# A graph kernel's gather stage: count matrices made four sets ahead instead of two, and gates of groups worked one by one in one PSUM bank

## The chip, the cores and the metric

The kernel runs on one core of a Trainium2 chip. The metric is the device time of the whole program in microseconds, the median of several runs. The kernel before took 1409.13 us (three runs: 1401.07, 1409.13 and 1409.19).

## The reference

The reference takes 6250 nodes of 256 features (`x`) and 100000 edges, sorted by one end (`src`, `dst`). Cut to what matters:

```python
xn = _layernorm(x)
agg = segment_sum(xn[nbr], dst, num_segments=n)          # _L0_gnn_ref
cnt = segment_sum(ones, dst, num_segments=n)
mean = agg / maximum(cnt, 1.0)[:, None]
gnn = xn @ W1.T + b1 + mean @ W2.T + b2
x = x + gnn + mix(xn)                                    # _L0_mix_ref: linear attention, 8 heads
h = _layernorm(x)
logits = h @ gate_w + gate_b                             # _L0_ffn_ref: 8 experts, top 1
idx, prb = argmax(softmax(logits)), its probability
pos = place of the token in its expert's list (running count); kept = pos < 977
x = x + expert_idx(h) * prb * kept                       # relu(h @ w1 + b1) @ w2 + b2
```

So there is a sum over each node's neighbours, then a layer norm, a choice of one of eight experts per node ("gate"), a running count per expert that gives each node its place, and the experts' two matrix products on the nodes sorted by expert.

## The kernel before, in words

**Three parts in time.** The first part (up to about 290 us of the span) sorts the edges' numbers, takes the first layer norm, makes the mixer's part of the result and writes for each node a row `z` to the table `z_d` in HBM. The second is the gather stage, with the gates beside it (to about 1019 us). The third (about 1050 us to the end) is the experts, 24 pairs of tiles of 128 nodes. Between the second and the third a short stretch makes the table of places (`pick`, `plc`, `idx_s`).

**One block of the gather stage.** The 6250 nodes are 49 tiles of 128. Block `b` sums the neighbours of the nodes of tile `b` in one PSUM tile `pa` (two buffers) by matmuls, in two ways:

- Of most edges both ends are known as classes. 24 columns (`J0 = 24`) of 128 z rows lie in SBUF as `z_s`. For each column a 128 x 128 *count matrix* says how often each row of it is a neighbour of each of the block's nodes. The function `counts` makes four at a time, one *set*, so six sets per block: four bf16 matmuls of one-hot matrices (`on`, `od`, made by DVE in `hot_classes`, two blocks ahead) into the PSUM tile `pc` (L911; one bank, two buffers), and one copy by ACT to SBUF as `cn` (L914; three buffers). `add_rows` then multiplies each count matrix with its column: two matmuls, L818 of 258 columns and L819 of 256. A set gives eight of these.
- The edges left over come as nine tiles of 128 gathered rows (`GT = 9`): POOL issues one indirect DMA for each (L901) from `z_d` into one of 19 buffers `zb`, and `add_rows` multiplies each with a one-hot matrix `og`. A buffer comes free, and POOL issues the next gather for it, once PE has read it.

**The order around the change.** The code writes one list of work, and a planner in the framework orders each engine's instructions by its own estimates of when their inputs are ready, so that the order on an engine is near, but not equal, to that of the code. Each engine then works through its list in order, and waits where an input or a buffer is not there. In the code, block `b` makes six turns `q`. A turn adds the gathered tiles due so far, issues new gathers, takes the oldest set `cn` from the list `cns`, makes the counts of the set **two** turns ahead (`j0 + 8`, in the next block if need be), adds the set's rows, and then takes one step of several side works: the next block's own rows (`own_steps`), the one-hot matrices of block `b + 2` (`hot_classes`, every other turn) and the gates.

**Gates.** After the last block of a group of seven tiles (the last seven in groups of four, two and one, so groups 6, 7 and 8) `gate_pieces` is begun as a generator, and each turn but the fifth takes one step of **every** generator that is open. Per tile of the group: norm on DVE, two transposes on PE into `ph` (L991), a copy to `hT` by ACT (L994), the logits' two small matmuls into `lgp` (L999). Then for the group: softmax and choice on DVE, two matmuls for the running count into `rkp`, DVE arithmetic of the places, one-hot matrices `pa_`, `pb_`, and matmuls that sum the table of places, which DVE adds to `places`. Before the change `lgp`, `rkp` and the places' sum are parts of a tile `lgr` with two buffers, and `ph` is a tile of its own, in the PSUM pool `lps`: three banks. After the last block what is left of the open generators is run to its end.

**PSUM.** The gather stage holds, in banks: `pa` two, `lane_p` (a row of numbers that DVE compares with) one, `pc` two, `lgr` two and `ph` one.

**Inputs of a block.** For each block, `inputs` loads two blocks ahead the node's own x (`xt`, ACT's queue), the mixer's part (`y`, ACT's queue) and `ov` (SP's queue). The places of a group lead to two stores on SP's queue (`buf_d` and `out`).

Of the kernel before, what the change touches and what calls it, by code (L numbers as in the profile page):

```python
# [7 lines left out]
F32 = mybir.dt.float32  # L8
BF16 = mybir.dt.bfloat16
F32R = mybir.dt.float32r  # L10
# [6 lines left out]
P = 128  # L17
# [4 lines left out]
G = 7  # L22
NG = NT // G
# [28 lines left out]
J0 = 2 * ND  # L52
# [13 lines left out]
NE, F = 8, 1024  # L66
FC = F // P
CAP = 977
ET_ = -(-CAP // P)
SP_ = ET_ // 2  # L70
NS = 32
S0 = 24
EPS = 1e-5
NZ = 19
OWN = 0.4
MIX = 0.74
# [9 lines left out]
def gnn_mix_moe_kernel(ctx: ExitStack, tc: tile.TileContext, x, src, dst, w1t, b1g, w2t, b2g,  # L86
                       kw, kb, vw, vb, gate_w, gate_b, fw1, fb1, fw2, fb2, out):
    nc = tc.nc
# [47 lines left out]
    eps = const.tile([P, 1], F32, name="eps")  # L136
    nc.vector.memset(eps, EPS)

# [36 lines left out]
    with tc.tile_pool(name="early", bufs=1) as ep, tc.tile_pool(name="work", bufs=2) as wp, \  # L175
# [136 lines left out]
        def finish(g, u):  # L312
# [399 lines left out]
        for q in range(1, QL + 1):  # L712
# [4 lines left out]
            c, o = (ep.tile([P, SG, R], F32, name=n) for n in ("s_i", "d_i"))  # L717
# [4 lines left out]
            for e in range(2):  # L722
                if q < 4:
                    b = slice(4 * e, 4 * e + 4)
                    pv, pw = pn[:, b, r0:r0 + R], pr[:, b, r0:r0 + R]
                else:
                    b = slice(e, SG, 2)
# [4 lines left out]
                if nb:  # L732
# [3 lines left out]
                    t = ce[:, :, :s].rearrange("p g (m q) -> p g m q", q=B)  # L736
# [16 lines left out]
            while j:  # L753
# [107 lines left out]

    with tc.tile_pool(name="gather", bufs=1) as ap_, tc.tile_pool(name="gwork", bufs=2) as wp, \
            tc.tile_pool(name="gps", bufs=1, space=bass.MemoryType.PSUM) as pp:
        tl_ = ExitStack()
        lane_p = pp.tile([P, 2 * P], F32, name="lane_p")
        nc.vector.tensor_copy(lane_p, iot)

# [28 lines left out]
        def gathers():  # L896

            nonlocal asked
            while asked < min(used + NZ, NB * GT):
                b, t = divmod(asked, GT)  # L900
                nc.gpsimd.indirect_dma_start(  # L901
                    out=zb[asked % NZ].bitcast(F32)[:, :DZ], out_offset=None, in_=z_d,
                    in_offset=bass.IndirectOffsetOnAxis(ap=idx[:, t, b:b + 1], axis=0))
                asked += 1

        def counts(b, j0):
            n = min(4, J0 - j0)
            on, od = ons[b % 2], ods[b % 2]
            pc = pp.tile([P, 4, P], F32, name="pc", bufs=2)
            for j in range(j0, j0 + n):  # L910
                nc.tensor.matmul(pc[:, j - j0, :], on[:, j // 2, (j % 2) * P:(j % 2 + 1) * P],  # L911
                                 od[:, j // 2, :], start=True, stop=True, skip_group_check=True)
            cn = wp.tile([P, 4, P], F32R, name="cn", bufs=3)
            nc.scalar.copy(cn[:, :n, :], pc[:, :n, :])  # L914
            return cn


        ebase = const.tile([P, NT + 1, NE], F32, name="ebase")
        nc.vector.memset(ebase[:, 0, :], 0.0)
        lp = tl_.enter_context(tc.tile_pool(name="lps", bufs=1, space=bass.MemoryType.PSUM))  # L920

        groups = [(g * G, G) for g in range(NG - 1)] + [(NT - 7, 4), (NT - 3, 2), (NT - 1, 1)]
        group_of = [k for k, (_, n) in enumerate(groups) for _ in range(n)]
        tokens, xts, ovs, ys, gate = {}, {}, {}, {}, {}
        LG = 3 * G * NE
        places = const.tile([P, 2 * NE * ET_], F32, name="places")
        nc.vector.memset(places, 0.0)

# [38 lines left out]
        def gate_pieces(k):  # L969
# [5 lines left out]
            rs = wp.tile([P, G], F32, name="rs")  # L975
            nc.scalar.activation(rs[:, :n], mv[:, :n, 1], AF.Sqrt, bias=eps)
            nc.vector.reciprocal(rs[:, :n], rs[:, :n])
            lgr = lp.tile([P, LG + 2 * NE * ET_], F32, name="lgr", bufs=2)
            lgp = lgr[:, :G * NE].rearrange("p (t e) -> p t e", e=NE)
            rkp = lgr[:, G * NE:LG].rearrange("p (i c) -> p i c", i=2)  # L980
            ph = lp.tile([P, 2, P], F32, name="ph")

            def norm(t):
                nc.vector.tensor_scalar(hn[:, t, :], row[:, t, D:2 * D], mv[:, t, 0:1], rs[:, t:t + 1],
# [4 lines left out]
            for t in range(n):  # L989
                for c in range(2):  # L990
                    nc.tensor.transpose(ph[:, c, :], hn[:, t, c * P:(c + 1) * P], ident)  # L991
                yield
                hT = wp.tile([P, 2, P], F32, name="hT", bufs=1)
                nc.scalar.copy(hT, ph)  # L994
                if t + 1 < n:
                    norm(t + 1)
                yield
                for c in range(2):
                    nc.tensor.matmul(lgp[:, t, :], hT[:, c, :], gw[:, c, :], start=(c == 0), stop=(c == 1),  # L999
                                     skip_group_check=True)  # L1000
# [75 lines left out]
            pb_ = wp.tile([P, G, 2, nt], BF16, name="pb_", bufs=1)[:, :n]  # L1076
# [1 line left out]
            nc.vector.tensor_tensor(pb_[:, :, 1, :], pe_, tnum[:, gs, None].to_broadcast([P, n, nt]), op=OP.mult)  # L1078
            yield
            for t in range(n):  # L1080
                nc.tensor.matmul(lgr[:, LG:], pa_[:, t, :], pb_[:, t].rearrange("p a c -> p (a c)"), start=(t == 0),
                                 stop=(t == n - 1), skip_group_check=True)
            yield
            nc.vector.tensor_add(places, places, lgr[:, LG:])

            if full:
                nc.sync.dma_start(out[g0 * P:(g0 + full) * P, :].rearrange("(t p) d -> p t d", p=P),
# [6 lines left out]
            return next(gen, 1) is None  # L1094

        gathers()
        for b in range(2):
            for part in range(3):
                hot_classes(b, part)
                if not b and part < 2:  # L1100
                    cns = cns + [counts(0, 4 * part)] if part else [counts(0, 0)]
            if not b:
                hot_gathered(0)
            inputs(b)
            if not b:
                for _ in own_steps(0):
                    pass
        for b in range(NB):

            nx, n2 = b + 1, b + 2  # L1110
            if n2 < NB:
                inputs(n2)
            og = ogs.pop(b)
            own_ = own_steps(nx) if nx < NB else iter(())
            pa = pp.tile([P, AW], F32, name="pa", bufs=2)
            t0, begun = 0, False
            for q, j0 in enumerate(range(0, J0, 4)):
                t1 = GT * (j0 + 4) // J0 if j0 + 4 < J0 else GT
                if not b:
                    t1 = (0, 0, 2, 4, 7, GT)[q]  # L1120
                for t in range(t0, t1):
                    add_rows(pa, og[:, t, :], zb[(b * GT + t) % NZ], not begun, False)
                    begun = True
                t0 = t1
                used = b * GT + t1
                gathers()
                cn = cns.pop(0)
                if j0 + 8 < J0:
                    cns.append(counts(b, j0 + 8))
                elif nx < NB:  # L1130
                    cns.append(counts(nx, j0 + 8 - J0))
                for j in range(j0, min(j0 + 4, J0)):
                    add_rows(pa, cn[:, j - j0, :], z_s[:, j, :], not begun, j == J0 - 1)
                    begun = True

                step(own_)
                if q % 2 == 0 and n2 < NB:
                    hot_classes(n2, q // 2)
                if q == 1 and nx < NB:
                    hot_gathered(nx)  # L1140
                for k in sorted(gate) if q != 4 else ():
                    if not step(gate[k]):
                        del gate[k]
            meaned(b, pa)
            k = group_of[b]
            if b + 1 == sum(groups[k]):
                gate[k] = gate_pieces(k)
        for k in sorted(gate):
            for _ in gate[k]:
                pass  # L1150
        tl_.close()

    zs_.close()
    with tc.tile_pool(name="table", bufs=1) as tp, tc.tile_pool(name="wgt", bufs=3) as wgt, \
# [26 lines left out]
        nt = NE * ET_  # L1181
# [146 lines left out]
```

## Time and profile before

| what | value |
|---|---|
| median of three runs | 1409.13 us |
| the profiled execution, its own time | 1408.68 us |
| span of that execution in the profile | 1406.9 us |
| PE busy with matmuls | 1131.7 us (80%) |
| DVE busy | 862.0 us (61%) |
| POOL busy | 534.4 us (38%) |
| ACT busy | 438.5 us (31%) |
| moved by DMA | 269.91 MB, mean 192 GB/s |

PE is TensorE's matmuls, PEld its weight loads (which run beside the matmuls), DVE is VectorE, ACT ScalarE, POOL GpSimd and SP the engine that only issues DMAs. A line such as "L911 PE MATMUL pc<-od,on ... x1144 | 121.3, 229 | 72.7 <-ACT cn L914 40.4" is a group of like instructions: the code's line, the engine, the operation, the tile written and those read, the shapes and the number of them; then their busy time in us and the mean of one in ns; then the time that the engine was idle just before them, and what ended most of it (here the copy of line 914, for 40.4 us of the 72.7). "Issue" is idle time for which the profile shows no other work that ended it. Ends of matmuls are modelled, and the time of one PE instruction as recorded overlaps with the next, so that the spacing of starts is the better measure of pace. "Granted clock" is the share of full speed at which the chip lets PE run.

### The profile page before, as it was taken

To read this page: it belongs to the slowest core of one execution; us is meant where nothing else is said; L and a number is where in the kernel's file an instruction comes from. 1 tells how busy PE (TensorE), PEld (TensorE's weight loads), DVE (VectorE), ACT (ScalarE), POOL (GpSimd) and SP (SyncE) were. 2 spreads that over 40 slices of the span, in tenths; PEclk is the share of its full clock that TensorE was granted. 3 is DMA by queue.
4 is the path that set the end of the run, shared out by engine and by line. 5 is a ranking of instruction groups with operands and counts; after the bars stand their busy time and mean duration, and the time that the engine had idled before them with its cause. 6 is when DMAs were issued, how large, how long until landed. Compare 5 with 4: busy or idle time off the path is not lost.

```text
span 1406.9 us, 21023 instructions
## 1 busy us (share of the span) xinstructions
PE 1131.7 (80%) x7471; PEld 1015.0 (72%) x7471; DVE 862.0 (61%) x2198; ACT 438.5 (31%) x954; POOL 534.4 (38%) x586
## 2 busy tenths in 40 slices
PE   0688968546879879779878889778829999999997
PEld 0577756346768778679768778778828888888886
DVE  8999877564657756666665666856633344343434
ACT  0677734212223222232232233233412322222231
POOL 0000011065665565555565556566121323222221
PEclk9999989868999899899899889999959999999999
DMA  9665213366676976866876966976573756666550
GB/s 252 198 230 177 96 48 119 101 196 193 203 229 187 226 221 197 237 210 184 246 220 179 252 201 189 252 211 196 154 269 129 226 186 214 216 200 226 182 202 21
DMA packets 147804, 269.91 MB, mean 192 GB/s; under 512 B 19139, under 2 KB 92557, under 8 KB 147692
## 3 DMA queue, kind: packets, MB, share of 16 engines
q0 software_dynamic: 42048, 134.90, 30.9%
q1 hardware_dynamic: 75431, 105.44, 24.8%
q10 hardware_dynamic: 30213, 28.15, 7.1%
q8 instruction: 61, 1.00, 0.3%
q14 instruction: 51, 0.42, 0.1%
HBM read 217.11 MB, written 52.21 MB: 191 GB/s over the span
## 4 chain that ended last, share of the span: by engine, by line
PE 62%; issue 7%; DVE 4%; another core or an unknown queue 2%; DMA 2%; ACT 2%; ACTq 0%; POOL 0%; DVEq 0%; POOLq 0%
PE pa L818 15%; PE pa L819 14%; PE pu L1234 12%; PE pd L1243 12%; PE pc L911 6%; PE lgr L999 2%; ACT cn L914 1%; PE ph L991 1%; DMA y<-y_d 1%; PE pB L1223 1%; DMA bt<-buf_d,idx_s 1%; DVE on L884 0%; DMA xt<-in_x_dram 0%; DVE row L954 0%
## 5 line engine op out<-in xcount | busy, mean ns | idle before, releaser
L901 POOL DMA_INDIRECT zb<-z_d,idx x441 | 422.9, 959 | 287.6 <-PE pa L819 86.5
L818 PE MATMUL pa<-z_s,cn 128*128 128x258 f32 x1176 | 344.3, 320 | 12.8 <-issue 12.5
L819 PE MATMUL pa<-z_s,cn 128*128 128x256 f32 x1176 | 321.3, 299 | 11.3 <-issue 11.0
L914 ACT CAST cn<-pc 128x512 fp32r<-128x512 f32 x294 | 171.7, 587 | 493.0 <-PE pa L819 177.0
L819 PEld LDWEIGHTS pa<-z_s,cn 128*128 128x128 f32 x1176 | 242.9, 207 | 17.1 <-issue 16.4
L818 PEld LDWEIGHTS pa<-z_s,cn 128*128 128x128 f32 x1176 | 242.8, 206 | 12.1 <-issue 11.8
L884 DVE TENSOR_TENSOR on<-lane_p,nvl 128x1024 bf16<-128x1024 f32 x147 | 178.7, 1216 | 80.6 <-PE pa L819 50.2
L911 PE MATMUL pc<-od,on 128*128 128x128 bf16 x1176 | 125.6, 230 | 81.6 <-ACT cn L914 40.4
L1235 ACT ACTIVATE hm<-pu,b1e 128x256 f32<-128x256 f32 x192 | 91.1, 474 | 266.0 <-PE pu L1234 238.6
L1243 PE MATMUL pd<-w2e,hm 128*128 128x256 f32 x768 | 173.3, 379 | 0.0
L1234 PE MATMUL pu<-bT,w1e 128*128 128x256 f32 x768 | 172.9, 383 | 0.0
L1234 PEld LDWEIGHTS pu<-bT,w1e 128*128 128x128 f32 x768 | 145.1, 191 | 26.8 <-issue 7.7
L1243 PEld LDWEIGHTS pd<-w2e,hm 128*128 128x128 f32 x768 | 144.1, 190 | 18.6
L911 PEld LDWEIGHTS <-on 128*128 128x128 bf16 x1176 | 78.7, 102 | 105.7 <-issue 84.8
L1257 POOL DMA_INDIRECT out_dram<-lim,tki_s x48 | 48.4, 1008 | 253.9 <-DVE lim L1256 245.6
L1246 DVE TENSOR_TENSOR yt<-pd,b2e 128x256 f32<-128x256 f32 x48 | 20.4, 425 | 192.6 <-PE pd L1243 192.6
L818 PE MATMUL pa<-zb,og 128*128 128x258 f32 x441 | 130.4, 308 | 8.4 <-issue 7.0
L819 PE MATMUL pa<-zb,og 128*128 128x256 f32 x441 | 125.3, 296 | 9.6 <-issue 9.4
L886 DVE TENSOR_TENSOR od<-lane_p,sll 128x512 bf16<-128x512 f32 x147 | 99.8, 679 | 0.0
L818 PEld LDWEIGHTS pa<-zb,og 128*128 128x128 f32 x441 | 90.1, 204 | 11.4 <-issue 8.5
L819 PEld LDWEIGHTS pa<-zb,og 128*128 128x128 f32 x441 | 90.3, 205 | 8.9 <-issue 8.9
L961 DVE TENSOR_TENSOR ov<-ov,pa 128x258 f32<-128x258 f32 x49 | 20.6, 420 | 106.8 <-PE pa L819 43.4
(382 smaller groups left out, 1477.4 us busy)
## 6 DMA issues: line engine op xcount, KB each, us to landing
w1e<-in_fw_dram SPq DMA_DIRECT2D x24, 1024.0 KB
w2e<-in_fw_dram SPq DMA_DIRECT2D x24, 1024.0 KB
z_d<-zr SPq DMA_DIRECT2D x49, 256.0 KB
buf_d<-row SPq DMA_DIRECT2D x6, 1795.5 KB
zb<-z_d,idx POOLq DMA_INDIRECT x441
ovf_d<-zero ACTq DMA_DIRECT2D x1, 6321.0 KB
ov<-ovf_d SPq DMA_DIRECT2D x49, 129.0 KB
y_d<-xg ACTq DMA_DIRECT2D x7, 896.0 KB
```

Of the source, the lines that this page charges most:

```text
L818: nc.tensor.matmul(ps[:, :AW], lhsT, z[:, D:], start=first, stop=False, skip_group_check=True)
L819: nc.tensor.matmul(ps[:, :D], lhsT, z[:, :D], start=False, stop=last, skip_group_check=True)
L884: nc.vector.tensor_tensor(ons[b % 2][:, c, :], lane_p[:, None, :].to_broadcast([P, n, 2 * P]), nv.to_broadcast([P, n, 2 * P]), op=OP.is_equal)
L886: nc.vector.tensor_tensor(ods[b % 2][:, c, :], lane_p[:, None, :P].to_broadcast([P, n, P]), sl.to_broadcast([P, n, P]), op=OP.is_equal)
L901: nc.gpsimd.indirect_dma_start(out=zb[asked % NZ].bitcast(F32)[:, :DZ], out_offset=None, in_=z_d, in_offset=bass.IndirectOffsetOnAxis(ap=i ...
L911: nc.tensor.matmul(pc[:, j - j0, :], on[:, j // 2, (j % 2) * P:(j % 2 + 1) * P], od[:, j // 2, :], start=True, stop=True, skip_group_check ...
L914: nc.scalar.copy(cn[:, :n, :], pc[:, :n, :])
L999: nc.tensor.matmul(lgp[:, t, :], hT[:, c, :], gw[:, c, :], start=(c == 0), stop=(c == 1), skip_group_check=True)
L1234: nc.tensor.matmul(pu, w1e[:, c, f * P:(f + 1) * P], bT[:, c, :], start=(c == 0), stop=(c == 1))
L1235: nc.scalar.activation(hms[s][:, f, :], pu, AF.Relu, bias=b1e[:, f:f + 1])
L1243: nc.tensor.matmul(pd, hm[:, f, j * P:(j + 1) * P], w2e[:, f, :], start=(f == 0), stop=(f == FC - 1))
L1257: st = nc.gpsimd.indirect_dma_start(out=out, out_offset=bass.IndirectOffsetOnAxis(ap=tki_s[:, 2 * s + j:2 * s + j + 1], axis=0), in_=lim, ...
```

## The change

Two things are changed together, since PSUM has eight banks.

The count matrices are made four sets ahead instead of two (`AHEAD = 4`): `pc` has four buffers instead of two and `cn` five instead of three, the four first sets are made ahead of block 0, and turn `q` makes the set at `j0 + 16` instead of `j0 + 8`.

The gates' PSUM shrinks from three banks to one. One tile `lgr` with one buffer, made once, holds the logits `lgp`, the running counts `rkp` and the transposes `ph`; the places' sum goes into `ph` too. Each turn now takes a step of the **earliest** open generator alone, so that no two groups are in work at once. The addition to `places` follows its matmuls in the same step, and for groups 0 to 4 (`k < NG - 2`) one more `yield` stands between the copy `hT` and the logits, one turn more per tile.

The lines of the changed kernel stand one to three further down than those of the kernel before. Cut to the core:

```diff
+AHEAD = 4
@@ counts
-            pc = pp.tile([P, 4, P], F32, name="pc", bufs=2)
+            pc = pp.tile([P, 4, P], F32, name="pc", bufs=AHEAD)
...
-            cn = wp.tile([P, 4, P], F32R, name="cn", bufs=3)
+            cn = wp.tile([P, 4, P], F32R, name="cn", bufs=AHEAD + 1)
@@ ahead of the gates
-        lp = tl_.enter_context(tc.tile_pool(name="lps", bufs=1, space=bass.MemoryType.PSUM))
+        lgr = pp.tile([P, 3 * G * NE + 2 * P], F32, name="lgr")
+        LG = 3 * G * NE
+        lgp = lgr[:, :G * NE].rearrange("p (t e) -> p t e", e=NE)
+        rkp = lgr[:, G * NE:LG].rearrange("p (i c) -> p i c", i=2)
+        ph = lgr[:, LG:].rearrange("p (c q) -> p c q", c=2)
@@ gate_pieces
-            lgr = lp.tile([P, LG + 2 * NE * ET_], F32, name="lgr", bufs=2)
-            lgp = lgr[:, :G * NE].rearrange("p (t e) -> p t e", e=NE)
-            rkp = lgr[:, G * NE:LG].rearrange("p (i c) -> p i c", i=2)
-            ph = lp.tile([P, 2, P], F32, name="ph")
...
                 if t + 1 < n:
                     norm(t + 1)
                 yield
+                if k < NG - 2:
+                    yield
                 for c in range(2):
                     nc.tensor.matmul(lgp[:, t, :], hT[:, c, :], gw[:, c, :], start=(c == 0), stop=(c == 1),
                                      skip_group_check=True)
...
-                nc.tensor.matmul(lgr[:, LG:], pa_[:, t, :], pb_[:, t].rearrange("p a c -> p (a c)"), start=(t == 0),
+                nc.tensor.matmul(ph[:, 0, :2 * nt], pa_[:, t, :], pb_[:, t].rearrange("p a c -> p (a c)"), start=(t == 0),
                                  stop=(t == n - 1), skip_group_check=True)
-            yield
-            nc.vector.tensor_add(places, places, lgr[:, LG:])
+            nc.vector.tensor_add(places, places, ph[:, 0, :2 * nt])
+            yield
@@ ahead of block 0
+        cns = []
...
-                if not b and part < 2:
-                    cns = cns + [counts(0, 4 * part)] if part else [counts(0, 0)]
+                if not b and part < AHEAD // 2:
+                    cns += [counts(0, 8 * part), counts(0, 8 * part + 4)]
@@ in a turn
-                if j0 + 8 < J0:
-                    cns.append(counts(b, j0 + 8))
+                ja = j0 + 4 * AHEAD
+                if ja < J0:
+                    cns.append(counts(b, ja))
                 elif nx < NB:
-                    cns.append(counts(nx, j0 + 8 - J0))
+                    cns.append(counts(nx, ja - J0))
...
-                for k in sorted(gate) if q != 4 else ():
+                for k in sorted(gate)[:1] if q != 4 else ():
```

More of the change, by code (lines that the diff above doesn't have):

```diff
@@ L863, in gnn_mix_moe_kernel @@
             tc.tile_pool(name="gps", bufs=1, space=bass.MemoryType.PSUM) as pp:
-        tl_ = ExitStack()
         lane_p = pp.tile([P, 2 * P], F32, name="lane_p")
@@ L926, in gnn_mix_moe_kernel @@
         tokens, xts, ovs, ys, gate = {}, {}, {}, {}, {}
-        LG = 3 * G * NE
         places = const.tile([P, 2 * NE * ET_], F32, name="places")
@@ L1150, in gnn_mix_moe_kernel @@
                 pass
-        tl_.close()
     zs_.close()
```

## The prediction

> **What bounds the kernel now.** I read the stage table first (busy time by stretch, with the granted clock), then the groups of instructions of the gather stage alone, then its waits, then a few microseconds of the timeline. The change touches only the gather stage, 316 to 1019 us of the span, and the short table stage behind it; the first 290 us and the 350 us of experts are untouched.
>
> Stretch, its length, then busy us of PE, PEld, DVE, ACT and POOL, granted clock, DMA share, GB/s:
>
> ```profile
> 316.00:391.00 75.00, 55.17 (x459) 51.45 (x459) 42.74 (x75) 16.98 (x30) 46.15 (x48) 0.93 0.67 200
> 391.00:1018.70 627.70, 518.26 (x4202) 488.29 (x4202) 411.25 (x928) 188.88 (x336) 355.60 (x371) 0.91 0.73 211
> ```
>
> No engine is full: PE is at 82%, DVE at 65%, POOL at 57%, ACT at 30%. So the stage is held by a loop between engines. The groups of the same stretch (busy and mean, then idle time before them and what ended it) say which:
>
> ```profile
> L901 POOL DMA_INDIRECT zb<-z_d,idx x419 | 401.8, 959 | 277.4 <-PE pa L819 83.0 <-issue 78.9 <-PE pc L911 59.7
> L818 PE MATMUL pa<-z_s,cn 128*128 128x258 f32 x1156 | 337.3, 319 | 12.1 <-issue 11.8
> L819 PE MATMUL pa<-z_s,cn 128*128 128x256 f32 x1156 | 314.7, 298 | 8.9 <-issue 8.6
> L914 ACT CAST cn<-pc 128x512 fp32r<-128x512 f32 x288 | 168.2, 587 | 451.4 <-PE pa L819 172.5 <-PE pc L911 153.0 <-remote 88.5
> L911 PE MATMUL pc<-od,on 128*128 128x128 bf16 x1144 | 121.3, 229 | 72.7 <-ACT cn L914 40.4 <-issue 31.4
> L999 PE MATMUL lgr<-gw,hT 128*128 128x8 f32 x188 | 28.4, 259 | 11.8 <-issue 10.8 <-ACT hT L994 0.9
> L991 PE MATMUL ph<-ident,row 128*128 128x128 f32 x96 | 22.3, 317 | 12.4 <-DVE row L984 7.6 <-DVE ov L961 4.3 <-DVE od L886 0.4
> ```
>
> PE's idle time is mostly in front of L911, the count matmuls: 72.7 us. They wait for ACT's copy of the set two before, which frees their PSUM buffer. ACT in turn is idle 451 us in front of that copy, waiting for PE. PE and ACT wait for each other with only two sets in flight. The timeline shows one turn:
>
> ```profile
> 360.51 0.59 ACT L914 CAST cn<-pc 128x512 fp32r<-128x512 f32 x1 [2.40 <-PE pc L911]
> 361.15 0.38 PE L911 MATMUL pc<-od,on 128*128 128x128 bf16 x4 [0.40 <-issue]
> 362.63 0.28 PE L818 MATMUL pa<-z_s,cn 128*128 128x258 f32 x1 [0.31 <-issue]
> 364.05 0.28 PE L819 MATMUL pa<-zb,og 128*128 128x256 f32 x1 [0.90 <-issue]
> 364.31 0.95 POOL L901 DMA_INDIRECT zb<-z_d,idx  x1 [1.41 <-PE pa L819]
> 364.52 1.09 ACT L914 CAST cn<-pc 128x512 fp32r<-128x512 f32 x2 [3.42 <-PE pa L819]
> 365.15 0.38 PE L911 MATMUL pc<-od,on 128*128 128x128 bf16 x4 [0.83 <-issue]
> ```
>
> The copy ends at 361.10 and L911 starts at 361.15; the next copies start at 364.52 and the next L911 at 365.15, just behind the first of the two. PE's news reaches ACT, DVE and POOL late and in bursts, microseconds after the recorded (modelled) ends of the matmuls. I do not know why; I use its size only. Taking the 294 copies in order with the 294 sets, the time from the end of a set's counts to the end of its copy is 2.0 us in the median, 4.1 at nine in ten, over 2.8 in 171 sets and over 5.8 in 14.
>
> **Part by part.** Instruction counts are the same on every engine; only orders and buffers differ. The sum is made against the profiled execution (1408.68 us; span 1406.9), which is 0.45 us under the median of 1409.13.
>
> *Four count sets ahead.* In the built PE order two sum sets and one count set stand between a set's counts and the next use of its bank: 22 sum matmuls at 0.117 us (their spacing at full clock) and four counts at 0.055, so 2.8 us. With four buffers it is 44 sums and twelve counts, 5.8 us. Copies late by that measure go from 171 of 294 to 14, and the time by which they are late from 266 to 33 us, 12%. L911's 72.7 us thus keep 12%, 9 us: **minus 64**. Bounds: minus 73 if all goes; nothing if the lag grows with the lead. What is late next is POOL. Back to back its gathers take 0.96 + 0.30 = 1.26 us, nine per block 11.3 us, while a block takes about 14.45 now (48 blocks between 325 and 1019). That leaves 48 x 3.1 = 150 us of room, so POOL stops the gain only beyond twice my figure. DVE's class matrices are needed two sets sooner: they are ready 17 us ahead in the median and 8.4 at the second percentile, less about 5, so still in time.
>
> *The clock.* Mean clock is 0.91 to 0.93. Sums stand 0.117 us apart at times and 0.21 at others (median record 284 ns, longest 562), so I read two levels, full and half. Half level then holds for 2 x 0.09 x 628 + 2 x 0.07 x 75 = 123 us, and costs up to 123 x (1 - 0.117/0.21) = 55 us. The half-level stretches follow PE waits. With most waits gone I take somewhat under half: **minus 25**, between 0 and minus 55.
>
> *Gates.* L999 and L991 wait 24 us in all. The added yield lets DVE's next norm and ACT's hT copy run further ahead of PE, but in the built order of the changed kernel the logits still stand within 0.6 us of PE work of their transposes in about half of the 49 tokens. I take **minus 8**, between minus 20 and plus 94 (the rival below). The places sum now waits for PE inside one step, which holds DVE nine times; DVE's lead in class matrices covers that (a few us if not).
>
> *New waits.* POOL and DMA come nearer to full (DMA 0.73 x 14.45/12.7 = 0.83). Between 0 and 30; **plus 10**.
>
> *Tail.* Groups 6, 7 and 8 end the stage. Now group 7 makes five steps beside block 48, and group 6 has only its last add left behind it. One by one, group 6's rank arithmetic on DVE (1012.1 to 1015.2, 3.1 us), its one-hot matrices (1015.2 to 1016.9, 1.7) and group 7's two turns of transpose, copy and logits (about 1.5 us each) follow block 48's last sum. Nothing hides them there: the experts' first fetch needs the places, and SP and POOL wait with it. **Plus 8**, between 4 and 12.
>
> Sum: -64 - 25 - 8 + 10 + 8 = -79, so 1408.7 - 79 = **1330 us**. A block would take about 12.6 us, above POOL's 11.3.
>
> The Trainium skill has two rules that speak against this, and the sum goes by neither. "TensorE: Matmul & The Clock Gate", section "HAM oscillation — how this bites in real kernels", reports a kernel in which PSUM double-buffering brought no further gain; taken as a rule it would leave only the tail, 1417 us. That section tells of a matmul kernel that had waited for its data by DMA; the rows above have PE waiting for ACT's copy out of PSUM. "PSUM — Partial Sum Buffer", section "PSUM bank collisions raise a hardware error", says two engines must not touch one bank at once, so sharing a bank forces order; that would add waits if two groups were in work, and by it the gates' 8 us would be lost, 1338 us.
>
> **Rivals.**
> - *POOL becomes the pace.* If the waits were one loop and all of it opens, a block falls to POOL's 11.3 to 11.9 us: 1408.7 - 150 + 8 = 1267, up to 1295. For it: gate-free blocks near 350 us take 13.6 us, of which POOL is busy or issuing 11.3. Against it: PE also stalls in the middle of sums, with no copy involved (0.90 us at 364.05).
> - *The wait only moves.* If the late news is a stop of PE itself, with recorded starts merely running ahead, more lead buys nothing: L911's 73 us reappear in front of L818 and L819 as "issue", and the tail is added: 1400 to 1417. This is also the case in which the change does not do what it says. For it: PE's restart at 364.05 falls together with the news to ACT and POOL. Against it: blocks of 11.4 us occur beside blocks of 19.
> - *The gates take it back (slower).* With one group in work and everything in one bank, each of the 49 tokens could make PE wait for ACT between transposes and logits, with the rest of PE's queue behind it. Such a wait is 2.1 us of idle time before L999 near 633 us. At 2.4 us per token, lag included, it is 118 us, 94 more than now, against -71 from the other parts: 1408.7 + 23 = 1432. It decides from 95 us, 1.9 us per token, where today's mean is 0.5.
>
> **How the numbers follow.** The forecast's case (1295 to 1395) has 0.66, POOL's pace 0.14, the moved wait 0.08, the slower one 0.12. The range for 8 in 10 leaves out the far end of POOL's pace, the slower case and part of the moved wait: 1270 to 1402. A change under 1% can hardly be told from none here: faster 0.80, same 0.08, slower 0.12.
>
> **What would show it.** Right: idle before L911 under 15 us; the gather stage near 615 us; POOL's idle "issue" share up and its waits for PE down; clock near 0.95; 7 to 9 us more between the last sum and the first fetch of bt. Wrong: "issue" before L818 and L819 up by as much as L911 loses, L999 and L991 above 50 us, or POOL back to back with PE waiting for zb.

## The result, and the profile after

The changed kernel takes **1413.27 us** in the median of 20 runs (1400.29 to 1427.24), the kernel before 1404.46 us (20 runs, 1393.51 to 1409.22). The ratio is 1.0064, with a 95% interval of 1.0039 to 1.0088: slower by 0.6%, where 1330 us had been forecast. On another chip, further down, the ratio was 1.0142 (1.0111 to 1.0172). The profiled execution of the changed kernel is one of its quicker ones, 1404.03 us (span 1402.2), which matters when its stages are added up.

The groups of the gather stage of the changed kernel (busy and mean, then idle time before them and what ended it; the window is that of the prediction, so here it takes in the first 14 us of the tail, too):

```profile
L901 POOL DMA_INDIRECT zb<-z_d,idx x419 | 401.0, 957 | 258.1 <-issue 84.8 <-PE pa L820 65.4 <-PE pc L911 62.3
L819 PE MATMUL pa<-z_s,cn 128*128 128x258 f32 x1156 | 337.6, 319 | 13.1 <-issue 12.5
L820 PE MATMUL pa<-z_s,cn 128*128 128x256 f32 x1156 | 313.9, 298 | 17.7 <-issue 17.2
...
L914 ACT CAST cn<-pc 128x512 fp32r<-128x512 f32 x286 | 166.9, 586 | 418.8 <-PE pc L911 173.8 <-PE pa L820 115.5 <-remote 80.2
...
L911 PE MATMUL pc<-od,on 128*128 128x128 bf16 x1140 | 123.7, 231 | 20.0 <-issue 18.0 <-ACT cn L914 2.0
...
L1001 PE MATMUL lgr<-gw,hT 128*128 128x8 f32 x192 | 31.2, 270 | 20.4 <-ACT hT L994 19.1 <-issue 1.3
```

The wait that the change was to remove is gone: L911 stood 72.7 us before, 40.4 of them behind ACT's copy, and now 20.0 and 2.0. The sums (L819, L820 here, L818 and L819 before) wait 31 us for "issue" in place of 21, and the logits (L1001) 19 us for ACT. A new wait is in the list of waits, in front of the places' matmuls; its columns are the time in all, the number and the longest:

```profile
PE lgr L1083 <- DVE pb__9827 L1080: 8.7, 1, 8.7
PE lgr L1083 <- DVE pb__4499 L1080: 7.0, 1, 7.0
```

The stage table has the columns of the prediction's. First the stretch behind the last sum of the kernel before:

```profile
1018.70:1050.00 31.30, 5.95 (x31) 3.69 (x29) 15.15 (x98) 3.65 (x6) 7.60 (x8) 0.56 0.72 241
```

Then the changed kernel's gather stage and the stretch behind it:

```profile
390.00:1005.00 615.00, 509.45 (x4165) 478.88 (x4164) 404.30 (x905) 183.64 (x329) 352.17 (x369) 0.90 0.71 212
1005.00:1045.00 40.00, 9.37 (x41) 6.01 (x40) 18.89 (x120) 3.12 (x7) 7.57 (x8) 0.54 0.68 208
```

PE's granted clock is as before (0.91 then, 0.90 now). From the last sum to the experts' first matmul it is 40.2 us in place of 31.6, 8.6 more. From the first sum to the last it is 717.0 us in place of 729.6 in these two executions; but this execution lies 9 us under its median and that of before 4 us over its own, so, carried over to the medians, the stage is as long as it was within a microsecond, and the 8.6 us of the tail are the difference.

So the question is where some 60 us of removed waiting went. A turn of the changed kernel, from its timeline (start, duration; in brackets the idle time before it):

```profile
349.59 0.59 ACT L914 CAST cn<-pc 128x512 fp32r<-128x512 f32 x1 [1.66 <-PE pc L911]
...
349.97 0.28 PE L820 MATMUL pa<-z_s,cn 128*128 128x256 f32 x1
...
350.93 0.28 PE L820 MATMUL pa<-z_s,cn 128*128 128x256 f32 x1 [0.56 <-issue]
...
352.36 0.28 PE L820 MATMUL pa<-z_s,cn 128*128 128x256 f32 x1 [1.02 <-issue]
...
352.59 0.59 ACT L914 CAST cn<-pc 128x512 fp32r<-128x512 f32 x1 [2.42 <-remote]
...
352.67 0.94 POOL L901 DMA_INDIRECT zb<-z_d,idx  x1 [1.34 <-remote]
```

PE all but stands still from 350.4 to 352.4 in the middle of a set's sums, at matmuls for which the profile names no releaser; the counts that it had issued at 349.56 to 349.96 are copied by ACT only at 352.59. ACT and POOL are idle for it and go on together when it does.

### The profile page after: what moved, and what is told of

It reads as the page before. It is cut to its first block, busy times and chain, and to the rows that moved or that the text cites. A ratio compares the mean times of both kernels' runs of the same rounds, so it can differ in the third digit from the quotient of the medians.

```text
span 1402.2 us, 21005 instructions
## 1 busy us (share of the span) xinstructions
PE 1134.1 (81%) x7471; PEld 1013.4 (72%) x7471; DVE 859.3 (61%) x2198; ACT 434.7 (31%) x952; POOL 533.3 (38%) x586
## 3 DMA queue, kind: packets, MB, share of 16 engines
q1 hardware_dynamic: 75431, 105.44, 24.2%
## 4 chain that ended last, share of the span: by engine, by line
PE 62%; DVE 6%; issue 5%; another core or an unknown queue 3%; DMA 2%; ACT 1%; POOL 0%; ACTq 0%; POOLq 0%; DVEq 0%
PE pa L819 14%; PE pa L820 13%; PE pu L1237 12%; PE pd L1246 12%; PE pc L911 6%; PE lgr L1001 2%; PE lgr L991 1%; DVE on L884 1%; DMA xt<-in_x_dram 1%; PE pB L1226 1%; DMA y<-y_d 1%; DVE og L891 1%; DMA bt<-buf_d,idx_s 1%; ACT cn L914 1%
## 5 line engine op out<-in xcount | busy, mean ns | idle before, releaser
L819 PE MATMUL pa<-z_s,cn 128*128 128x258 f32 x1176 | 344.7, 320 | 14.8 <-issue 14.2
L820 PE MATMUL pa<-z_s,cn 128*128 128x256 f32 x1176 | 320.8, 299 | 21.3 <-issue 20.8
L819 PEld LDWEIGHTS pa<-z_s,cn 128*128 128x128 f32 x1176 | 242.2, 206 | 22.8 <-issue 22.5
L820 PEld LDWEIGHTS pa<-z_s,cn 128*128 128x128 f32 x1176 | 242.6, 206 | 20.9 <-issue 20.7
L911 PE MATMUL pc<-od,on 128*128 128x128 bf16 x1176 | 129.0, 232 | 34.3 <-issue 23.4
L819 PE MATMUL pa<-zb,og 128*128 128x258 f32 x441 | 130.3, 308 | 4.4 <-issue 2.5
L820 PE MATMUL pa<-zb,og 128*128 128x256 f32 x441 | 126.1, 298 | 4.5 <-issue 4.1
L965 DVE TENSOR_TENSOR ov<-ov,pa 128x258 f32<-128x258 f32 x49 | 20.5, 419 | 176.7 <-PE pc L911 88.7
L911 PEld LDWEIGHTS <-on 128*128 128x128 bf16 x1176 | 74.3, 104 | 55.7 <-issue 34.5
L820 PEld LDWEIGHTS pa<-zb,og 128*128 128x128 f32 x441 | 90.7, 206 | 6.4 <-issue 6.4
L819 PEld LDWEIGHTS pa<-zb,og 128*128 128x128 f32 x441 | 90.7, 206 | 6.0 <-issue 3.7
```

What stands on the lines that cost most here:

```text
L819: nc.tensor.matmul(ps[:, :AW], lhsT, z[:, D:], start=first, stop=False, skip_group_check=True)
L820: nc.tensor.matmul(ps[:, :D], lhsT, z[:, :D], start=False, stop=last, skip_group_check=True)
```

## The experiments

The experiments ran on five chips (A to E here), and these differ: the kernel before took 1408.58, 1419.29, 1282.82, 1406.18 and 1282.23 us on them. So each ratio is to runs of the kernel before on the same chip, and C and E are told of by themselves.

### Chip A: which part of the change costs what

**gates_alone.** All of the change but the lead.

```diff
-AHEAD = 4
+AHEAD = 2
```

> The gates' part of the change alone: counts two sets ahead, as before, and the gates in one bank, one group at a time, with the extra yield. Theory 1 (the gates' new order costs what the counts' lead gains: in the changed kernel DVE's one-hot matrices for the places stand behind the add that ends a block, and PE waits 24 us for them inside the stage, 9 us more for the rank and 8 us more for the logits): the kernel before plus about 35 us plus 8.6 us of tail, about 1445 us, ratio 1.03, and PE's waits ahead of the places' matmuls above 20 us. Theory 2 (the lead gains nothing, because the waits of L911 were PE's own stops and come back ahead of the sums; only the tail is added): plus 8.6 us, 1413 us, ratio 1.006.

Measured: 1413.17 us, ratio 1.0041 (1.0014 to 1.0069). The tail is 39.3 us. Theory 1 falls as it was priced (1445 us): with two sets the gates' new order costs its tail and no more.

**counts_alone.** The lead, with the gates' steps as before save that one group is worked at a time.

```diff
-                if k < NG - 2:
-                    yield
...
-            nc.vector.tensor_add(places, places, ph[:, 0, :2 * nt])
             yield
+            nc.vector.tensor_add(places, places, ph[:, 0, :2 * nt])
```

> The counts four sets ahead alone, as far as PSUM lets it: the gates stay in one bank and one group at a time, but without the extra yield and with the add to places one step after its matmuls, as before the change. Theory 1: the waits for the places, the rank and the logits fall back to what they were before, about 35 us less than the changed kernel: about 1378 us, ratio 0.98. Theory 2: the same as the changed kernel, 1410 to 1415 us, ratio 1.004 to 1.008.

Measured: 1415.33 us, ratio 1.0068 (1.0038 to 1.0098), tail 40.0 us. The lead without the gates' extra step gains nothing either, as theory 2 has it. PE's waits for the places' one-hot matrices are there all the same (7.6 us the longest), so the extra step is not what brings them.

PE's idle time from 316 us to the last sum, added up by what ended it (worked out from the same traces as the views), for these and for the pair on chip D:

| kernel | counts for ACT's copy | issue, all lines | gates for DVE or ACT | all |
|---|---|---|---|---|
| before | 40.7 | 72.0 | 15.1 | 129.3 |
| gates_alone | 19.2 | 69.3 | 32.9 | 122.1 |
| counts_alone | 0.0 | 75.2 | 47.3 | 123.9 |
| after | 2.0 | 61.0 | 53.2 | 117.7 |
| tail_mended (below) | 0.5 | 82.8 | 28.8 | 113.0 |
| before, chip D | 38.7 | 71.6 | 13.8 | 124.6 |
| after, chip D | 0.4 | 78.9 | 47.1 | 128.9 |

The waits for the copy fall from 40 us to 19 and to nearly none, and the sum falls by 5 to 16 us only, or rises (chip D): PE waits in other places. That suggests that something else gives the stage its length.

**loads_sp.** On the changed kernel, the loads that stand among the copies in ACT's queue.

```diff
-            load_x(xts[b], b, 1, nc.scalar)
+            load_x(xts[b], b, 1, nc.sync)
...
-            nc.scalar.dma_start(ys[b], y_d[b * P:(b + 1) * P, :])
+            nc.sync.dma_start(ys[b], y_d[b * P:(b + 1) * P, :])
```

> The changed kernel with the loads of xt and y issued by SP in place of ACT. Theory 3 (PE's stops ahead of the sums, named issue, and the late news to ACT come with ACT's issues of these loads, which stand ahead of the copies in ACT's queue): the issue waits of L819 and L820 (some 50 us) fall by half or more and the time by about 25 us, to 1388 us. If these loads have no part in it: 1413 us, within 5 us.

Measured: 1408.87 us, ratio 1.0001 (0.9973 to 1.0028), by the ratios 9 us less than the changed kernel where theory 3 asked for 25. PE's issue waits add up to 60.2 us, as they were (61.0). The loads have a small part at most (the changed kernel's ratio is from another chip); theory 3 falls.

**tail_mended.** counts_alone, and:

```diff
+            own = pp.tile([P, 4 * P], F32, name="pc", bufs=AHEAD) if k > NG - 1 else lgr
+            lgp = own[:, :G * NE].rearrange("p (t e) -> p t e", e=NE)
...
-                for k in sorted(gate)[:1] if q != 4 else ():
+                for k in [k for k in sorted(gate) if k > NG - 1 or k == min(gate)] if q != 4 else ():
```

> counts_alone, with the last two groups of gates in PSUM buffers of their own (two of the count matrices' buffers, which are free by then), stepped beside the others. The tail from the last sum to the experts' first matmul was 31.7 us before and 40.3 us in the changed kernel. If the one by one makes the tail longer: 4 to 9 us less than counts_alone, tail 32 to 36 us. If not: the same as counts_alone.

Measured: 1407.20 us, ratio 0.9992 (0.9965 to 1.0019), tail 33.3 us: 8 us less than counts_alone; the tail's own part is 6.7. So the tail is what makes the changed kernel slower, and with it mended four sets ahead cannot be told from two. Nor do the gates take the gain back here: copies and gates together wait 29 us in place of 56 before, and the time is the same.

### Chip B: whose pace is it?

A block of the stage with no gate beside it (there are five or six in a row near 340 us) takes 13.4 us in the changed kernel, measured from the add that ends one block (L965) to the next (the first of them, shortened by the head start, left out). Each of the next four takes one kind of work away from the changed kernel.

**sums_fewer.**

```diff
-                for j in range(j0, min(j0 + 4, J0)):
+                for j in range(j0, min(j0 + 4, J0)) if q != 2 else ():
```

> The changed kernel with one set of count matrices in six left out of the sums (eight sum matmuls of 66 per block; the set is still made and copied). Theory 4 (PE's own work is the pace of the stage: a block without gates takes 13.4 us for 66 sums and 24 counts, so about 0.17 us per sum and 0.09 per count if the time goes by columns, and the starts in the profile run ahead of the work): 49 x 8 x 0.17 = 67 us less than the changed kernel, about 1346 us, ratio 0.957. Theory 5 (POOL's gathers or the DMA behind them are the pace, PE waits for them in some way that the profile doesn't name): no change, 1413 us.

**cols_half.**

```diff
-        nc.tensor.matmul(ps[:, :D], lhsT, z[:, :D], start=False, stop=last, skip_group_check=True)
+        nc.tensor.matmul(ps[:, :D // 2], lhsT, z[:, :D // 2], start=False, stop=last, skip_group_check=True)
```

> The changed kernel with the second matmul of each sum over 128 columns in place of 256 (the other half of the low parts is left out); the number of matmuls and weight loads is the same. Theory 4 with the time going by columns: 33 x 128 columns fewer of 16,962 + 3,072 per block, a fifth, 2.8 us of 13.4, until POOL's 11.3 us per block bounds it: 100 us less, about 1310 us, ratio 0.93. Theory 4 with the time going by instructions (each matmul with its own weight load): no change, within 10 us. Theory 5: no change.

**counts_half.**

```diff
-            for j in range(j0, j0 + n):
+            for j in range(j0, j0 + n // 2):
```

> The changed kernel with two count matmuls per set in place of four (the copy doubles the two, so the sums use a wrong half of the count matrices; the number of sums is the same). Theory 4: 12 counts fewer per block at 0.09 us, 49 x 12 x 0.09 = 53 us less, about 1360 us, ratio 0.967; at the 0.055 us that the starts stand apart, 32 us less. Theory 5: no change.

**gathers_fewer.**

```diff
+                if t < GT - 1 or b < 3:
                     nc.gpsimd.indirect_dma_start(
```

> The changed kernel with eight gathers per block in place of nine from block 3 on (the ninth tile's sums run on rows gathered earlier), so a ninth less for POOL and about a ninth less for DMA, and the same work for PE. Theory 4: no change, 1413 us within 6. Theory 5: 46 x 1.25 = 58 us less, 1355 us, ratio 0.96.

| kernel | us | ratio to before (interval) | blocks without gates, us |
|---|---|---|---|
| sums_fewer | 1432.50 | 1.0121 (1.0043 to 1.0199) | 13.4 to 13.5 |
| cols_half | 1405.40 | 0.9899 (0.9869 to 0.9929) | 10.5 to 17.1, mean 14.2 |
| counts_half | 1416.80 | 0.9980 (0.9947 to 1.0013) | 12.1 to 14.9, mean 13.8 |
| gathers_fewer | 1375.48 | 0.9714 (0.9653 to 0.9775) | 12.2 to 13.0 |

Set against the changed kernel's own ratio (1.0064; it did not run on this chip), an eighth of the sums is worth nothing, half of the second matmuls' columns 1.7% (23 us of the 100 asked for), half of the counts 0.8% (12 us of 53), and one gather in nine 3.5%, 50 us of the 58 asked for (against the ratio that the changed kernel has on chip D, 1.0142, each would be 11 us more). In sums_fewer PE's freed time comes back as waiting, in front of the counts and with no releaser:

```profile
L911 PE MATMUL pc<-od,on 128*128 128x128 bf16 x1107 | 122.6, 239 | 84.7 <-issue 58.1 <-DVE od L886 10.2 <-ACT cn L914 8.3
```

For the blocks without gates theory 4 falls: an eighth of the sums less leaves them at 13.4 us, and the two kernels with less work of another kind do not shorten them either (where those gain their 23 and 12 us stays open). One gather less does: the length of a block goes by the number of gathers, 13.4 / 9 = 1.49 us each and 12.2 / 8 = 1.53, while POOL can issue one every 1.26 (0.96 and 0.30 of idle time). But PE does not wait for the rows, as theory 5 has it, and POOL is not the bound. By the times of the gathers' DMA packets, PE reads a gathered tile some 20 us after its last packet (median from 340 to 400 us: 20.5 in the kernel before, 19.6 in the changed one, in the profiles of the result), and POOL itself waits for PE to free a buffer. So the gathers hold the block by their presence, not by coming late.

### Chip C: without the stops

**nz_12.**

```diff
-NZ = 19
+NZ = 12
```

> The changed kernel with 12 buffers for gathered rows in place of 19, so POOL may run 12 gathers ahead of PE's release and no more. Theory 6 (POOL is the pace of the stage: nine gathers per block at 1.25 us, 11.3 us, and two stops of about one us; a block without gates takes 13.4 us in all kernels with nine gathers, whatever work PE has, and 12.2 with eight), and gathered rows lie ready some 18 us before PE reads them: about 8 us are left, no change, 1413 us within 8. If POOL's stops for a free buffer are the pace themselves (a loop of gather, use and release over the buffers): the loop has 12 in place of 19 buffers, and the stage grows by 100 us or more.

**gathers_thin.**

```diff
-                    out=zb[asked % NZ].bitcast(F32)[:, :DZ], out_offset=None, in_=z_d,
+                    out=zb[asked % NZ].bitcast(F32)[:, :D], out_offset=None, in_=z_d.rearrange("r (h c) -> (r h) c", h=2),
```

> The changed kernel with gathers of 1 KB per row in place of 2 KB: as many gathers, half their bytes (the rows read are meaningless and their second half is zero; the sums run over them all the same; DVE clears the buffers once, ahead of the stage). Theory 6a (POOL's issuing of a gather is the pace): no change, a block without gates 13.4 us. Theory 6b (the bytes that DMA moves are the pace: 2.75 MB per block is 205 GB/s at 13.4 us, and 2.49 MB at 12.2 us with eight gathers is 204 GB/s): 1.18 MB less per block, so up to 5.7 us less, until POOL's 11.3 us bounds it: about 100 us less.

**after_g5** and **before_g5**, on the changed kernel and on the one before:

```diff
+                if t < 5 or b < 3:
                     nc.gpsimd.indirect_dma_start(
```

> The changed kernel with five gathers per block in place of nine from block 3 on (the other four tiles' sums run on rows gathered earlier; PE's work is the same). Theory 6: the block falls to what comes next, PE: 66 sums at 0.117 us and 24 counts at 0.055, 9.0 us and some clock, so 10 to 10.5 us without gates and 130 to 150 us less than the changed kernel, about 1275 us. If PE is held by something other than the gathers: 1360 us or more.

> The kernel before with five gathers per block in place of nine from block 3 on, to be set against after_g5. Theory 6: with POOL out of the way the wait of the counts for their copies decides, and the four sets' lead is worth what was forecast for it: this kernel is 30 to 60 us slower than after_g5. If the lead is worth nothing in any case: 8 us faster than after_g5, by the tail.

This chip runs the kernel before in 1282.82 us. Measured: nz_12 1288.80 us, ratio 1.0038 (1.0019 to 1.0058); gathers_thin 1285.55, 1.0032 (1.0005 to 1.0059); after_g5 1219.97, 0.9496 (0.9477 to 0.9515); before_g5 1214.00, 0.9441 (0.9414 to 0.9468). In none of the four does PE have issue waits in the stage. With nine gathers, blocks without gates are about 11.4 us where they have settled (10.7 to 11.8 in nz_12): nine at 1.26, POOL's own pace. Half of the bytes and 12 buffers change little or nothing there: both ratios are no higher than the longer tail alone gives (1.006; the changed kernel itself did not run on this chip). For chips with the stops neither of the two says anything.

With five gathers both kernels' blocks are 9.6 us, and before_g5 is the faster of the two by 6 us, about what its shorter tail (31.9 us against 39.9) gives it. So with POOL out of the way the lead is still worth nothing on such a chip: without the stops the copies are in time with two sets as well (the counts wait 3.7 us in before_g5).

### Chip D: the two kernels and the gathers, on one chip with the stops

**before_again** and **after_again** are the two kernels unchanged; **after_g5_again** is after_g5; **after_g0** has `if b < 3:` in its place.

> The kernel before once more, with a profile on the same chip as the three that follow. Theory 7 (the counts' wait for ACT's copy is the shadow of PE's own stops: PE stands still for 2 to 4 us with no releaser, its updates come late, the copy comes late, and the record puts part of the stop down to the copy): on a chip with the stops (about 1409 us) the waits of L911 are about 70 us and issue about 60 us; on a chip without them (about 1283 us) both are under 10 us.

> The changed kernel once more on the same chip. Theory 7: 4 to 10 us slower than before on either chip, by the tail of 8.6 us; stage within 8 us of that of before. Theory of the prediction (the counts' wait is PE's own loss): faster by 50 us where the waits are.

> Five gathers per block from block 3 on, as in after_g5. If the stops come with the gathers: on a chip with the stops the issue waits of PE fall from 60 us to 35 or less and the stage to below 560 us. If they come from PE's own work or its instructions: the issue waits stay at 55 us or more. On a chip without stops: as after_g5, ratio 0.95.

> No gathers from block 3 on (all sums of gathered tiles run on rows gathered in the first blocks; PE's work is the same). If the stops come with the gathers: no issue waits are left on any chip, and the stage takes what PE's work takes, about 10 us per block. If not: 55 us or more of issue waits on a chip with the stops.

Measured: before_again 1407.90 us; after_again 1426.77, ratio 1.0142 (1.0111 to 1.0172); after_g5_again 1250.88, 0.8889 (0.8843 to 0.8935); after_g0 1232.01, 0.8762 (0.8729 to 0.8795). From the first sum to the last the two kernels take 725.4 and 725.7 us in their profiled executions; the tail is 31.6 and 39.4. (Their medians lie 19 us apart, 11 more than the tail and more than theory 7 allowed; of that the profiles show nothing, and that of after_again is of its quickest run, 1414.37 us.) PE's groups in the stage, from 316 us to its end, before_again first:

```profile
L818 PE MATMUL pa<-z_s,cn 128*128 128x258 f32 x1158 | 339.9, 321 | 6.3 <-issue 6.2
L819 PE MATMUL pa<-z_s,cn 128*128 128x256 f32 x1157 | 316.4, 300 | 10.4 <-issue 9.2
...
L911 PE MATMUL pc<-od,on 128*128 128x128 bf16 x1152 | 123.3, 232 | 73.2 <-ACT cn L914 38.3 <-issue 33.9
```

after_again:

```profile
L819 PE MATMUL pa<-z_s,cn 128*128 128x258 f32 x1159 | 336.4, 317 | 20.3 <-issue 20.0
L820 PE MATMUL pa<-z_s,cn 128*128 128x256 f32 x1159 | 312.0, 296 | 15.8 <-issue 15.4
...
L911 PE MATMUL pc<-od,on 128*128 128x128 bf16 x1140 | 122.8, 230 | 21.2 <-issue 20.5 <-ACT cn L914 0.4 <-DVE od L886 0.2
```

after_g5_again:

```profile
L819 PE MATMUL pa<-z_s,cn 128*128 128x258 f32 x1156 | 317.6, 306 | 0.0
L820 PE MATMUL pa<-z_s,cn 128*128 128x256 f32 x1156 | 294.6, 285 | 0.0
...
L912 PE MATMUL pc<-od,on 128*128 128x128 bf16 x1140 | 113.6, 224 | 2.0 <-issue 2.0
```

L911 loses 52 us and the sums gain 20; with five gathers the sums wait for nothing and the counts 2.0 us (the gates' matmuls still 20), and the stage takes 563.2 us, where below 560 had been asked for. The stops go with the gathers: all issue waits of PE in the stage are 79 us with nine (after_again), 46 with eight (gathers_fewer, chip B), 3 with five and 0.5 with none. The table of stretches without gates, 340 to 400 us, shows the same from PE's side (its columns are again those of the stage table). after_again, after_g5_again and after_g0:

```profile
340.00:400.00 60.00, 49.09 (x408) 45.22 (x407) 40.13 (x72) 15.85 (x27) 39.05 (x41) 0.97 0.71 209
```

```profile
340.00:400.00 60.00, 60.00 (x563) 58.38 (x563) 53.48 (x98) 22.80 (x42) 28.57 (x30) 1.00 0.63 193
```

```profile
340.00:400.00 60.00, 60.00 (x563) 58.39 (x562) 52.77 (x97) 22.88 (x41) 0.00 (x0) 1.00 0.20 58
```

With nine gathers PE gets through 408 matmuls, with five or none through 563, at full clock and without a gap: 9.6 us per block is PE's own pace, and with five gathers it is the bound. POOL, with nine, stands idle for PE on this chip (139 us in all after_again's stage; the 84.3 of "issue" are nearly all its 0.3 us from one gather to the next):

```profile
L901 POOL DMA_INDIRECT zb<-z_d,idx x420 | 403.5, 961 | 263.2 <-issue 84.3 <-PE pa L820 74.8 <-PE pc L911 64.2
```

The late news goes with the gathers, too. From the end of a set's counts to the end of its copy it is 2.8 us in the median in before_again and 3.3 in after_again, and 0.7 in after_g5_again and after_g0. Four sets ahead did not make the news come sooner; fewer gathers did.

So theory 7 holds for the copies: the counts' wait was the shadow of the stops, 73.2 us where they are and (below, chip E) 2.1 where they are not. Less directly shown is that the gates' longer waits (13.8 to 47.1 us here) are the same stops and no price of the new order. Three quarters of the copies' 38.7 us come after 415 us of the span, about where the gates begin: in five blocks without gates they are 1.6 us with two sets and none with four, and both kernels take 67.1 us for the five. Against such a price speak gates_alone, and tail_mended, where the gates wait 14 us more than before, the counts 40 less, and nothing is gained.

### Chip E: is a better version to be had?

**both_mended** is tail_mended with loads_sp's edit, **before_loads_sp** the kernel before with it.

> tail_mended (counts four sets ahead, the gates' order as before, the last two groups of gates in banks of their own) with the loads of xt and y issued by SP. If the two gains add up: ratio 0.999 - 0.006 = 0.993. If the loads' gain was the changed kernel's own (its order): 0.997 to 1.001.

> The kernel before with the loads of xt and y issued by SP. If ACT's queue held up the copies in both kernels alike: ratio 0.994, and then the lead is worth nothing on top. If only the changed kernel gains from it: 0.998 to 1.003.

Measured: both_mended 1282.14 us, ratio 1.0001 (0.9973 to 1.0028); before_loads_sp 1280.52, 0.9976 (0.9945 to 1.0008). Neither can be told from the kernel before on this chip, which has no stops. In its code before_loads_sp differs from the kernel before in these loads alone, so its profile shows what PE waits for on such a chip:

```profile
L818 PE MATMUL pa<-zb,og 128*128 128x258 f32 x424 | 126.3, 309 | 52.8 <-DMA zb<-z_d,idx 50.3 <-DVE row L984 1.1 <-DVE og L891 0.7
...
L911 PE MATMUL pc<-od,on 128*128 128x128 bf16 x1124 | 113.0, 224 | 2.1 <-ACT cn L914 2.0
```

Two sets in flight, and the counts wait 2.1 us in all. The copy ends 0.7 us after its counts in the median. What PE waits for is the gathers, and here the profile says so: it reads a gathered tile 0.9 us after its last packet (median, 340 to 400 us).

## Why the prediction was wrong

**The wait of the counts (minus 64).** As a forecast of the wait it was near: 72.7 us went to 20.0 (9 had been forecast), and the part behind ACT's copy to 2.0. It failed in the step that counted a removed wait as gained time: the stage gained nothing. The wait was a shadow: PE stood still, its news reached ACT late, the copy was late, and the profile put part of PE's stop down to the copy. With two more sets the copy no longer holds the counts, and PE's idle time stands in other places: 10 us more in front of the sums, 38 more in front of the gates' matmuls (that these 38 are the same stops is argued, not shown). The prediction's own rows had a sign: of the 72.7 us only 40.4 were put down to the copy, 31.4 were "issue", as were both L911 of its timeline, and the sum priced all of it. "I do not know why; I use its size only" was said of the late news, and that was the place to stop: an unexplained lag was used as if it were a property of the copy. (The lag's median and nine-in-ten figure, 2.0 and 4.1 us, cannot stand beside 171 of 294 sets over 2.8; taken again from the trace they are 3.2 and 5.5. The 171 and 14, on which the term rests, are right. ACT's share is 29%, not 30.)

**POOL's room (150 us).** The block was set against POOL's 11.3 us, and the 3.1 us left over were taken as room. On the chips with the stops a block without gates takes 13.4 us with nine gathers, an eighth of the sums less or not, and 12.2 with eight: 1.5 us per gather in place of 1.26. So there was no room, though POOL stood idle. That such blocks took 13.6 us again and again stood in the prediction, as a point for the rival of POOL's pace; so regular a time beside waits that vary from set to set was a hint of a pace from elsewhere.

**The clock (minus 25).** It was to follow the waits, and PE's idle time in all hardly fell (129.3 to 117.7 us; on chip D it rose, 124.6 to 128.9); the clock stayed at 0.90 to 0.91, where near 0.95 had been forecast.

**Gates (minus 8) and new waits (plus 10).** L999 and L991 waited 24.2 us before; their lines in the changed kernel wait about 30. The new waits were sought at POOL and DMA and came at the places' matmuls (7.0 and 8.7 us the longest). No price of either is seen: gates_alone and counts_alone have different waits and, within their intervals, the same time.

**The tail (plus 8).** Right: 8.6 us more here, 7.8 on chip D, and 6.7 given back by tail_mended. It is all that the profiles show of the loss.

**The rivals.** "The wait only moves" held, at 1400 to 1417 us, and had been given 0.08. Its reason, a stop of PE itself, fits the runs; its sign, all 73 us back in front of the sums, does not (10 us came there, 20 on chip D); what spoke against it, short blocks beside long ones, was no evidence, since it says nothing on who waits for whom. "POOL becomes the pace" had the right work and the wrong sign: the stage went by the gathers already, though not by POOL's issuing of them. "The gates take it back" asked for 1.9 us of waiting per token and for a price; waits came, the price was not seen.

The case that "TensorE: Matmul & The Clock Gate" in the Trainium skill reports (section "HAM oscillation — how this bites in real kernels"), a kernel in which double-buffering of PSUM brought no further gain, would have given 1417 us if taken as a rule. The measured 1413.27 agrees with it in size; the reason that the runs show here is the stops that come with the gathers.

## What to carry to other kernels

A wait is worth its time only if its end is what the stage waits for. Before a wait is priced, find out who sets the length of one turn: where turns last the same to a tenth of a microsecond while the waits in them vary, take work away from each engine in turn, and price only what belongs to the one that shortens the turn. Where one engine's news reaches several others late and at the same moment, the waits for it can be one stop that the profile shows in several places, and then another buffer only moves it.

## What the runs showed of the hardware that was not expected

- The same program takes 1282 to 1283 us on two chips and 1404 to 1419 on the others. The difference lies in the gather stage: 596.5 us from the first sum to the last (before_loads_sp) against 725.4 (before_again). The experts take 348 to 349 us on all of them, from their first matmul to their last.
- On the slower chips 2.2 to 3.6 us pass between two of PE's semaphore updates about three times per block without gates, PE has 61 to 79 us of waits with no releaser in the stage (two profiles of the changed kernel), and these vanish as gathers are taken away. On the faster chips there are none with all nine gathers, and DMA moves 257 GB/s in the stretch of 340 to 400 us (before_loads_sp) in place of 209 (after_again).
- What in a gather stops PE stays open. It is not late rows, which lie ready for some 20 us. In the stretches without gates of three profiles (326 to 415 us of before_again, after and after_again) 45 of 55 gaps of over 1.8 us between PE's semaphore updates end within 0.1 us of a landing of one of the gathers, where 31% of all moments lie so near to one. But 42 of the 55 begin as near to one, and seven in ten of all PE's updates are as near: on these chips PE's updates and the landings come in the same bunches, so it does not show that a landing ends a stop. The profile is also incomplete there: from 340 to 400 us it has 4.8 landing updates per gather in before_again and 16.2 in before_loads_sp, so "no releaser" may mean one that it did not catch. Fewer buffers and thinner gathers ran only on a chip without stops, so they do not settle it.
